# Cross attention: value products by head pairs, with high and low V columns in one stationary, and half of the softmax sums on VectorE

## The chip, the cores and the metric

One core of one Trainium2 chip runs the whole problem in one launch. The metric is device time in microseconds (us); lower is better.

## The reference

For each of 32 batches there are 512 queries of width 640 and 77 context rows of width 1024. Queries, keys and values are projected, 20 heads of 32 columns attend to the 77 context rows (all 77 are text rows, so the other branches of the original layer are empty), and the result is projected, with bias and residual added.

```python
q = heads(x @ to_q_w)                                   # (32, 20, 512, 32)
k, v = heads(ctx @ to_k_w), heads(ctx @ to_v_w)         # (32, 20, 77, 32)
s = einsum('bhqd,bhkd->bhqk', q, k) / sqrt(32)
p = softmax(s, axis=-1)
h = merge(einsum('bhqk,bhkd->bhqd', p, v))              # (32, 512, 640)
out = h @ to_out_w + to_out_b + x
```

## The kernel before

**Numbers.** All operands are fp32. TensorE multiplies fp32r values, so each operand is split into a high part (a cast to fp32r) and a low part (the rest), and a product is the sum of three: high by high, high by low, low by high. `PAIRS` lists them.

**Context stage.** The 2464 context rows are taken in five groups of 512 (the last has 416). For each group, keys and values of the five column chunks (128 columns, four heads each) are made with eight accumulation steps per chunk. `split_values` transposes a chunk of V in 32 by 32 blocks on VectorE (`vt`), splits it into high and low in the tile `vs` (two buffers: ScalarE casts, VectorE subtracts), and issues four DMAs to `v_dram` on SyncE's queue (L235). The order on ScalarE is that of the program: in groups 1 to 4, the casts of the next group's context (`ct`) of steps 1 and up stand behind the `vs` cast of chunk 3.

**Main stage.** A slot `n` handles one chunk `j` of one batch `b` (160 slots). The order of all engines is written out by hand in `slot`; every engine takes its instructions in that order. In a slot,
- TensorE makes four score tiles (`scores`, three matmuls each, t = 0 to 3, three PSUM buffers), the queries of the next slot (`queries`, 6 + 9 matmuls of 512 columns), the value product of slot n - 3 (`values`), and two pieces of output projection of the batch before (`piece`, 12 matmuls of 320 columns each).
- VectorE takes the negated row maxima of each score tile (`nm`, L482); ScalarE makes 16 exponentials of 128x77 with them (`exps`, L492), each of which also gives its row sum in `sm` by `accum_out`; VectorE inverts the sums of slot n - 1 (`rs`, L502); GpSimd multiplies (`pn`, L507); VectorE transposes (`z`, L514); SyncE stores `z` to `pd` (L521) and loads it back two slots later with keys on partitions (`raw`).
- ScalarE casts the probabilities of slot n - 3 (`pp`, L538 and L544), VectorE makes the low parts of their first 256 rows (L545), and GpSimd those of the last 64 rows (L552), which lie with their high parts in `pp[:, 4]`.
- `values` (L566) contracts over 320 rows: four heads of 80 padded keys. Its stationary `vb` is block diagonal: 128 rows by the 32 columns of each of four heads. It takes eight passes of 512 columns: three for rows 0 to 127, three for rows 128 to 255, and two for rows 256 to 319, where high and low probabilities share one operand, `pp[:, 4]`.
- `split_a` splits the product into `at` (ScalarE L104, VectorE L105), which the projection (`project`, L596) takes a batch later. VectorE adds the residual and bias, which GpSimd has added up in `xr` (L589), to a closed output bank (`finish`, L624).
- `transpose_x` (VectorE L257) and `split_x` (ScalarE L264, GpSimd L265) prepare the next batch's `x` in some of the slots: transposes after t = 1 in j = 1 and 2, transposes between the last score tile and `split_a` in j = 0 and 1, casts in j = 2 and 3.

The order at the end of a slot is this:

```python
        if taken is not None:
            values(taken)
        ...
            s = scores(n, 3)
        finish()
        for i in turns[1]:
            transpose_x(b + 1, i)
        if taken is not None:
            split_a(taken)
        for c in xsplits[1]:
            split_x(b + 1, c)
        exps(n, 3, *s)
```

The next slot begins with `cast_p` on ScalarE.

Of the kernel before, what the change touches and what calls it, by code (L numbers as in the profile page):

```python
# [23 lines left out]
P = 128  # L24
# [11 lines left out]
SEGMENTS = []  # L36
for _t in range(3):
    for _i in range(HPC):
        _lo = max(_t * P, _i * KPAD)
        _hi = min((_t + 1) * P, (_i + 1) * KPAD)  # L40
        if _lo < _hi:
            SEGMENTS.append((_t, _lo - _t * P, _i, _lo - _i * KPAD, _hi - _lo))
            if _t == 2:
                SEGMENTS.append((_t, _lo - _t * P + 64, _i, _lo - _i * KPAD, _hi - _lo))

# [5 lines left out]
def kernel(  # L51
# [46 lines left out]
    v_dram = dram.tile([NT + KPAD - NKEY, HPC, NC_, HD, 2], FPR, name="v_dram")  # L98
# [124 lines left out]
    def split_values(g, j, between=None):  # L223
# [7 lines left out]
        vs = kvp.tile([P, G // Q, HD, 2], FPR, tag="vs", name="vs", bufs=2)  # L231
        split(vs[:, :na, :, 0], vs[:, :na, :, 1], vt[:, :gn].rearrange("p (a d) -> p a d", d=HD))
        dst = v_dram[g0 : g0 + gn, :, j].rearrange("(a t) i d c -> i t a (d c)", t=Q)
        for i in range(HPC):
            nc.sync.dma_start(  # L235
                dst[i].bitcast(F32),
                vs[i * Q : (i + 1) * Q, :na].rearrange("p a d c -> p a (d c)").bitcast(F32),
            )
# [31 lines left out]

    zero = kvt.tile([P, 2, G], FPR, name="zero", tag="ks")[:, 0]
# [45 lines left out]
    def split_wo():  # L317
# [8 lines left out]
        v_dram[NT:].rearrange("n i j d a -> (n i j d a)").rearrange("(p u) -> p u", u=P).bitcast(F32),  # L326
        zero[: (KPAD - NKEY) * HEADS * HD * 2 // P, :P].bitcast(F32),
# [62 lines left out]
    raws, pps, ats, pds, sms, pqs, pas, xrs, pos = ({} for _ in range(9))  # L390
# [14 lines left out]
    for g, (j0, nj) in enumerate(GROUPS):  # L405
        vb = main.tile([P, nj, 3, HPC * HD, 2], FPR, name=f"vb{g}")
        nc.gpsimd.memset(vb.bitcast(F32), 0.0)
        vbs.append(vb)
# [12 lines left out]
    def load_values(b, g, segments=SEGMENTS):  # L421
        j0, nj = GROUPS[g]
        v = v_dram.rearrange("n i j d a -> n j i (d a)")
        for t, r0, i, k0, kn in segments:
            k0 += b * NKEY
            nc.sync.dma_start(
                vbs[g][r0 : r0 + kn, :, t, i * HD : (i + 1) * HD, :]
                .rearrange("p j d a -> p j (d a)")
                .bitcast(F32),
# [57 lines left out]
    def exps(n, t, sc, nm):  # L487
        if t == 0:
            sms[n] = main.tile([P, NQ * HPC], F32, tag="sm", name="sm", bufs=2)
        for i in range(HPC):  # L490
# [6 lines left out]
                accum_out=sms[n][:, at : at + 1],  # L497
            )

# [11 lines left out]
    def transpose_p(n):  # L511
# [6 lines left out]
        pd = dram.tile([NBLK * Q, S], F32, tag="pd", name="pd", bufs=6)  # L518
        rows = pd.rearrange("(b i) q -> i b q", i=Q)
# [7 lines left out]
    def load_p(n):  # L527
        pd = pds.pop(n)
        raw = late[0].tile([P, 3, S], F32, tag="raw", name="raw", bufs=2)
        nc.sync.dma_start(raw[:, 0:2, :], pd[0 : 2 * P, :].rearrange("(k p) q -> p k q", p=P))  # L530
        nc.sync.dma_start(raw[:64, 2, :], pd[2 * P :, :])
# [26 lines left out]
    PASSES = [(t, a, t + c * 2) for t in range(2) for a, c in PAIRS] + [(2, 0, 4), (2, 1, 4)]  # L558

    def values(n):  # L560
# [3 lines left out]
        pas[n] = late[1].tile([P, S], F32, tag="pa", name="pa", bufs=1)  # L564
        for m, (t, a, c) in enumerate(PASSES):
            nc.tensor.matmul(  # L566
                pas[n],
                vb[:, t, :, a],
                pp[:, c, :],
                start=(m == 0),  # L570
                stop=(m == len(PASSES) - 1),
            )

    def split_a(n):
# [4 lines left out]
        split(at[:, 0, :], at[:, 1, :], pas.pop(n))  # L579
# [11 lines left out]
    def output_bank(b, t, h):  # L591
        pos[b, t, h] = late[1].tile([P, S], F32, tag="po", name="po", bufs=3)
# [14 lines left out]
    STEPS += [(t, h, j) for t in range(1, NQ) for h in range(2) for j in range(NC_)]  # L607
    closed = []

    def piece(b, i):  # L610
        for t, h, j in STEPS[4 * i : 4 * i + 4]:
# [36 lines left out]
    def take(m):  # L648
        values(m)
        split_a(m)  # L650
# [248 lines left out]
```

## Time and profile before

| what | value |
| --- | --- |
| time, median of 3 runs (lowest to highest) | 1958.72 us (1957.45 to 1960.53) |
| span of the profiled execution, first to last instruction | 1956.4 us |
| mean granted TensorE clock | 0.997 |
| TensorE busy | 1929.6 us (99%) |
| ScalarE busy | 1596.1 us (82%) |
| VectorE busy | 1363.1 us (70%) |
| GpSimd busy | 1024.9 us (52%) |
| share of the 16 DMA engines, hardware queue of SyncE | 83.4% |

The profiled execution has no time of its own in the runs; its span is 2.3 us below the median of the runs, and that difference is taken for what lies around the span. The stretches of the profile are the context stage (0 to 262 us), the first slots, in which nothing is projected yet (262 to 396 us), the main stage (396 to 1915 us) and the end (1915 to 1957 us). "Idle before" in a row is the time in which that engine waited just before the instruction, and the arrow names what ended it.

### The profile page before, as it was taken

Reading aid. Unit: us, or ns where it says so; the run is one execution under the profiler, and the core shown is the slowest. Engines: PE = TensorE matmul, PEld = TensorE weight load, DVE = VectorE, ACT = ScalarE, POOL = GpSimd, SP = SyncE. Lnnn points to the kernel's source line nnn. Section 1 sums busy time; section 2 is a strip of 40 time slices with the busy share of each in tenths; the row PEclk is TensorE's granted clock in tenths of the full one; section 3 lists DMA queues with packets and bytes.
Section 4 is the critical chain, followed back from the end, with each engine's and each line's share of the span. In section 5 each row is a group of like instructions: output and inputs, shape, how many; then the busy total and the mean of one; then the engine's idle time right before and its main releaser. Section 6 shows DMA issues by size and latency. Waiting matters only on the chain.

```text
span 1956.4 us, 37549 instructions
## 1 busy us (share of the span) xinstructions
PE 1929.6 (99%) x10652; PEld 1727.8 (88%) x10652; DVE 1363.1 (70%) x2174; ACT 1596.1 (82%) x6370; POOL 1024.9 (52%) x688
## 2 busy tenths in 40 slices
PE   9999997999999999999999999999999999999999
PEld 7787895889989989999999999999999999998998
DVE  4444446677777777777777777777777777777774
ACT  3232248899999999999999999999999999999993
POOL 0211144566556555555555556655655565555555
PEclk9999999999999999999999999999999999999999
DMA  9877869988888889888988888888888888888876
GB/s 187 172 166 214 174 158 209 219 231 227 216 220 226 227 222 233 226 226 224 236 219 235 217 232 226 226 222 234 223 227 225 225 221 228 218 223 226 224 205 190
DMA packets 592537, 423.49 MB, mean 216 GB/s; under 512 B 219567, under 2 KB 501325, under 8 KB 592333
## 3 DMA queue, kind: packets, MB, share of 16 engines
q1 hardware_dynamic: 588461, 409.79, 83.4%
q0 software_dynamic: 3776, 11.15, 2.1%
q8 instruction: 88, 1.44, 0.3%
q14 instruction: 116, 0.95, 0.2%
q10 hardware_dynamic: 96, 0.16, 0.0%
HBM read 245.61 MB, written 175.32 MB: 215 GB/s over the span
## 4 chain that ended last, share of the span: by engine, by line
PE 86%; DMA 6%; SPq 2%; ACT 2%; DVE 2%; issue 2%; POOL 1%; ACTq 0%; DVEq 0%; POOLq 0%
PE po L596 27%; PE pq L439 26%; PE pa L566 14%; PE sc L474 10%; PE pk L192 5%; PE pv L192 4%; DMA raw<-pd 2%; DMA xs<-in_x_dram 1%; DMA pd<-z 1%; SPq L235 1%; DMA k_dram<-ks 1%; POOL pn L507 1%; ACT pp L538 0%; DMA v_dram<-vs 0%; ACT pn L492 0%
## 5 line engine op out<-in xcount | busy, mean ns | idle before, releaser
L492 ACT ACTIVATE pn<-sc,nm 128x77 f32<-128x77 f32 x2560 | 799.2, 329 | 45.2 <-DVE nm L482 32.4
L507 POOL TENSOR_TENSOR pn<-pn,rs 128x1232 f32<-128x1232 f32 x160 | 364.7, 2279 | 646.9 <-DVE rs L502 632.9
L596 PE MATMUL po<-wo_s,at 128*128 128x320 f32 x3840 | 625.9, 312 | 0.1
L439 PE MATMUL pq<-xt,wq_s 128*128 128x512 f32 x2400 | 619.3, 398 | 1.2 <-POOL xt L265 1.2
L596 PEld LDWEIGHTS po<-wo_s,at 128*128 128x128 f32 x3840 | 565.0, 188 | 0.7 <-DVE xr L624 0.3
L492 ACT ACTIVATION_READ_ACCUMULATOR pn<-sc,nm 128x1 f32 x2560 | 529.5, 207 | 0.0
L482 DVE TENSOR_REDUCE nm<-sc 128x4 f32<-128x308 f32 x640 | 294.2, 460 | 308.8 <-PE sc L474 303.9
L439 PEld LDWEIGHTS pq<-xt,wq_s 128*128 128x128 f32 x2400 | 428.4, 189 | 78.3 <-POOL xt L265 2.4
L566 PE MATMUL pa<-pp,vb 128*128 128x512 f32 x1280 | 329.3, 398 | 2.8 <-POOL pp L552 2.4
L566 PEld LDWEIGHTS pa<-pp,vb 128*128 128x128 f32 x1280 | 242.3, 196 | 43.0 <-POOL pp L552 5.3
L514 DVE STREAM_TRANSPOSE z<-pn 128x1280 f32<-128x1280 f32 x160 | 241.3, 1508 | 27.5 <-POOL pn L507 20.9
L545 DVE TENSOR_TENSOR pp<-raw,pp 128x1024 fp32r<-128x1024 f32 x160 | 196.1, 1226 | 71.3 <-ACT pp L538 63.9
L474 PEld LDWEIGHTS sc<-kc,qt 128*128 128x128 f32 x1280 | 211.6, 188 | 26.6 <-ACT qt L454 4.6
L552 POOL TENSOR_TENSOR pp<-raw,pp 64x512 fp32r<-64x512 f32 x160 | 210.5, 1316 | 42.5 <-ACT pp L544 30.6
L474 PE MATMUL sc<-kc,qt 128*128 128x154 f32 x1280 | 223.0, 255 | 4.1 <-DVE qt L456 2.1
L456 DVE TENSOR_TENSOR qt<-pq,qt 64x512 fp32r<-64x512 f32 x320 | 214.5, 670 | 11.7 <-ACT qt L450 7.3
L265 POOL TENSOR_TENSOR xt<-xs,xt 128x512 fp32r<-128x512 f32 x160 | 204.1, 1296 | 32.3 <-ACT xt L264 28.3
L589 POOL TENSOR_TENSOR xr<-xr,bias 128x640 f32<-128x640 f32 x128 | 201.2, 1573 | 9.7
L454 ACT CAST qt<-qt 64x512 fp32r<-64x512 f32 x320 | 198.1, 619 | 9.0
L474 PE MATMUL sc<-kb,qt 128*128 128x308 f32 x640 | 195.3, 305 | 7.4 <-ACT pn L492 6.2
L538 ACT CAST pp<-raw 128x1024 fp32r<-128x1024 f32 x160 | 170.2, 1064 | 17.3 <-DMA raw<-pd 17.1
L104 ACT CAST at<-pa 128x512 fp32r<-128x512 f32 x160 | 94.7, 592 | 75.8 <-PE pa L566 75.4
(44 smaller groups left out, 1542.5 us busy)
## 6 DMA issues: line engine op xcount, KB each, us to landing
pd<-z SPq DMA_DIRECT2D x640, 160.0 KB, 3.5
raw<-pd SPq DMA_DIRECT2D x160, 512.0 KB, 4.3
xs<-in_x_dram SPq DMA_DIRECT2D x128, 320.0 KB, 6.3
xr<-in_x_dram SPq DMA_DIRECT2D x128, 320.0 KB, 3.8
out_dram<-xr SPq DMA_DIRECT2D x127, 320.0 KB, 3.1
raw<-pd SPq DMA_DIRECT2D x160, 128.0 KB, 4.4
v_dram<-vs SPq DMA_DIRECT2D x80, 128.0 KB, 3.0
kc<-k_dram SPq DMA_DIRECT2D x128, 57.8 KB, 4.2
```

The source lines that it names most:

```text
L265: low.tensor_tensor(parts[1], src, parts[0].bitcast(F32), ALU.subtract)
L439: nc.tensor.matmul(pqs[n], wq_s[:, k, a, j * P : (j + 1) * P], xts[b, k][:, c, :], start=(k == 0 and m == 0), stop=(k == NC_ - 1 and m == 2),)
L456: nc.vector.tensor_tensor(qt[r, 1 + w, :], pq[r], qt[r, 0, :].bitcast(F32), ALU.subtract)
L474: nc.tensor.matmul(sc[:, cols], qt[:, m, t * P : (t + 1) * P], keys_, start=(m == 0), stop=(m == 2),)
L482: nc.vector.tensor_reduce(nm, sc[:, :KCOLS].rearrange("p (h k) -> p h k", k=NKEY), AX.X, ALU.max, negate=True)
L492: nc.scalar.activation(pnb[n % 2][:, at, :NKEY], sc[:, i * NKEY : (i + 1) * NKEY], AF.Exp, bias=nm[:, i : i + 1], accum_out=sms[n][:, at : ...
L507: nc.gpsimd.tensor_tensor(pf, pf, rs.unsqueeze(2).to_broadcast([P, NQ * HPC, NKEY]), ALU.mult)
L514: nc.vector.transpose(z.rearrange("p b t j -> p t b j"), pn.rearrange("p (t h) k -> p t (h k)", t=NQ).rearrange("p t (b i) -> p t b i", i=Q),)
L552: nc.gpsimd.tensor_tensor(pp[64:, 4, :], raw[:64, 2, :], pp[:64, 4, :].bitcast(F32), ALU.subtract)
L566: nc.tensor.matmul(pas[n], vb[:, t, :, a], pp[:, c, :], start=(m == 0), stop=(m == len(PASSES) - 1),)
L589: nc.gpsimd.tensor_tensor(xrs[b, t], xrs[b, t], bias, ALU.add)
L596: nc.tensor.matmul(pos[b, t, h][:, :HALF], ats[b * NC_ + j][:, a, t * P : (t + 1) * P], wos[0][:, j, c, h * HALF : (h + 1) * HALF], start= ...
```

## The change

1. **V by head pairs.** The 320 rows are regrouped into three sets of 128, 128 and 64: one set for heads 0 and 1, one for heads 3 and 2, and a shared set with the rest of heads 1 and 2. `vb` holds for each pair p a stationary of 128 columns: 64 of high and 64 of low V columns of the two heads. `values` takes three passes for each pair (high probabilities, low probabilities, shared set), six in all, into two PSUM banks (`pa`, 128 x 2 x 512); low by low is now part of the product. The third pass of the first pair reads `pp[:, 4]`.
2. **Adding the parts.** `sum_a`, new, copies the 64 low rows of `pa` (64 x 1024) to SBUF on ScalarE, and VectorE adds them to the high rows, two adds of 64x512. `split_a` casts from SBUF on ScalarE, and its subtraction goes from VectorE to GpSimd. It stands behind `exps(n, 3)`.
3. **Sums.** The exponentials of t = 0 and 1 no longer give sums; VectorE sums their 8 x 77 columns (`reduce_sums`, one reduction a slot, behind `sum_a`).
4. **Around it.** `vs` is one tile for the whole kernel in place of two buffers, with a zero column block between high and low, so `v_dram` rows are 96 numbers in place of 64. The output banks are two in place of three; the pieces of the projection are cut at other steps (`CUTS`), and in slots with j = 3 `finish` comes ahead of the last score tile too. `pd` has a gap of 64 rows so that `raw` lands in the new grouping.

```diff
-        vs = kvp.tile([P, G // Q, HD, 2], FPR, tag="vs", name="vs", bufs=2)
-        split(vs[:, :na, :, 0], vs[:, :na, :, 1], vt[:, :gn].rearrange("p (a d) -> p a d", d=HD))
+        split(vs[:, :na, 0], vs[:, :na, 2], vt[:, :gn].rearrange("p (a d) -> p a d", d=HD))
...
+    vs = kvp.tile([P, G // Q, 3, HD], FPR, name="vs")
+    nc.gpsimd.memset(vs.bitcast(F32), 0.0)
...
-        vb = main.tile([P, nj, 3, HPC * HD, 2], FPR, name=f"vb{g}")
+        vb = main.tile([P, nj, 2, 2, P], FPR, name=f"vb{g}")
...
                 bias=nm[:, i : i + 1],
-                accum_out=sms[n][:, at : at + 1],
-            )
+                **({} if t in REDUCED else dict(accum_out=sms[n][:, at : at + 1])),
+            )
+
+    REDUCED = (0, 1)
+
+    def reduce_sums(n):
+        k = len(REDUCED) * HPC
+        nc.vector.tensor_reduce(sms[n][:, :k], pnb[n % 2][:, :k, :NKEY], AX.X, ALU.add)
...
-    PASSES = [(t, a, t + c * 2) for t in range(2) for a, c in PAIRS] + [(2, 0, 4), (2, 1, 4)]
+    PASSES = [(p, t, c) for p in range(2) for t, c in ((0, p), (0, 2 + p), (1, 4))]
...
-        pas[n] = late[1].tile([P, S], F32, tag="pa", name="pa", bufs=1)
-        for m, (t, a, c) in enumerate(PASSES):
+        pas[n] = late[1].tile([P, 2, S], F32, tag="pa", name="pa", bufs=1)
+        for m, (p, t, c) in enumerate(PASSES):
             nc.tensor.matmul(
-                pas[n],
-                vb[:, t, :, a],
+                pas[n][:, p, :],
+                vb[:, p, t, :],
                 pp[:, c, :],
-                start=(m == 0),
-                stop=(m == len(PASSES) - 1),
+                start=(m % 3 == 0),
+                stop=(m % 3 == 2),
             )
+
+    def sum_a(n):
+        pa = pas.pop(n)
+        aw = late[0].tile([P, 2, S], F32, tag="aw", name="aw", bufs=1)
+        nc.scalar.copy(aw[:64], pa[64:])
+        for p in range(2):
+            nc.vector.tensor_tensor(aw[64 * p : 64 * p + 64, 0], pa[:64, p], aw[:64, p], ALU.add)
+        aws[n] = aw
...
-        split(at[:, 0, :], at[:, 1, :], pas.pop(n))
+        aw = aws.pop(n)
+        nc.scalar.copy(at[:, 0, :], aw[:, 0])
+        nc.gpsimd.tensor_tensor(at[:, 1, :], aw[:, 0], at[:, 0, :].bitcast(F32), ALU.subtract)
...
-        pos[b, t, h] = late[1].tile([P, S], F32, tag="po", name="po", bufs=3)
+        pos[b, t, h] = late[1].tile([P, S], F32, tag="po", name="po", bufs=2)
...
+    CUTS = (0, 4, 8, 10, 16, 20, 24, 28, 32, 36, 40)
...
             values(taken)
         ...
+        if j == 3:
+            finish()
         if has_out:
             s = scores(n, 3)
         finish()
         for i in turns[1]:
             transpose_x(b + 1, i)
         if taken is not None:
-            split_a(taken)
+            sum_a(taken)
+        reduce_sums(n)
         for c in xsplits[1]:
             split_x(b + 1, c)
         exps(n, 3, *s)
+        if taken is not None:
+            split_a(taken)
```

## The prediction

> **What bounds the kernel now.** I read the page first: busy times and the shares of the chain that ended last.
>
> ```profile
> PE 1929.6 (99%) x10652; PEld 1727.8 (88%) x10652; DVE 1363.1 (70%) x2174; ACT 1596.1 (82%) x6370; POOL 1024.9 (52%) x688
> ...
> PE 86%; DMA 6%; SPq 2%; ACT 2%; DVE 2%; issue 2%; POOL 1%; ACTq 0%; DVEq 0%; POOLq 0%
> ```
>
> TensorE is the bound, and by the stretches it is so in the main stage almost without a gap: 1518.14 us busy of the 1519 from 396 to 1915. The chain in order of time gives its price list:
>
> ```profile
> 1011.79 0.33 PE sc L474 x3
> 1012.11 1.80 PE po L596 x12
> 1013.91 1.87 PE pa L566 x8
> ```
>
> A value pass is 1.87 / 8 = 0.235 us, and a slot is 10.3 us (51.5 a batch). A shorter TensorE helps only if the other engines can follow, so I next read the timeline of one slot (j = 1), for the ring of waits that runs from one `pp` cast (L538) to the next.
>
> ```profile
> 1007.82 1.05 ACT L538 CAST pp<-raw 128x1024 fp32r<-128x1024 f32 x1
> ...
> 1008.90 1.23 DVE L545 TENSOR_TENSOR pp<-raw,pp 128x1024 fp32r<-128x1024 f32 x1 [0.35 <-ACT pp L538]
> ...
> 1010.04 0.25 DVE L502 RECIPROCAL rs<-sm 128x16 f32<-128x16 f32 x1
> ...
> 1010.43 2.28 POOL L507 TENSOR_TENSOR pn<-pn,rs 128x1232 f32<-128x1232 f32 x1 [5.22 <-DVE rs L502]
> ...
> 1012.74 1.51 DVE L514 STREAM_TRANSPOSE z<-pn 128x1280 f32<-128x1280 f32 x1
> 1012.79 1.29 POOL L552 TENSOR_TENSOR pp<-raw,pp 64x512 fp32r<-64x512 f32 x1
> 1013.75 2.04 PE L566 MATMUL pa<-pp,vb 128*128 128x512 f32 x8
> ...
> 1014.18 1.37 DVE L456 TENSOR_TENSOR qt<-pq,qt 64x512 fp32r<-64x512 f32 x2
> ...
> 1015.82 0.59 ACT L104 CAST at<-pa 128x512 fp32r<-128x512 f32 x1 [0.69 <-PE pa L566]
> ...
> 1016.15 0.48 DVE L482 TENSOR_REDUCE nm<-sc 128x4 f32<-128x308 f32 x1 [0.60 <-PE sc L474]
> 1016.66 0.49 DVE L624 TENSOR_TENSOR xr<-po,xr 128x320 f32<-128x320 f32 x1
> 1017.07 0.83 DVE L257 STREAM_TRANSPOSE xs<-xs 128x640 f32<-128x640 f32 x1
> ```
>
> In the middle of the list: the low part L552 is done at 1014.08, 0.3 us into the value passes, and only the last two of eight read it. The first `pp` cast to the end of that row takes 6.26 us, each step released by the one before. After it nothing in the ring is long today: `at` cast, exponentials of t = 3 (1.2 us, four at 0.30), next cast at 1017.88. TensorE has room over it because VectorE's part of `at` (L105) is not in the ring.
>
> **The change, part by part.** Its own time: span 1956.4, 2.3 us outside, median 1958.7. All differences are put on the median. I take start-to-start distances where steps follow each other.
>
> *Two passes fewer.* 2 x 0.235 = 0.47 us a slot of TensorE, 10.31 to 9.84, if TensorE stays the bound. The stage holds 1519 / 51.5 = 29.5 batches: -2.35 x 29.5 = -69 us.
>
> *The ring with the parts added.* Time 0 is the start of L538. From the rows above: L545 at 1.08, `rs` at 2.22, `pn` at 2.61, `z` at 4.92, L552 from 4.97 to 6.26. Now the third pass of six reads `pp[:, 4]`, so four passes, not two, stand behind L552: first pass to `at` cast was 2.07 us for eight, less 4 x 0.235 = 1.13, so `pa` is complete at 6.28 + 1.13 = 7.41. The 64x1024 PSUM copy is not in the trace. Between its neighbours, the 128x1024 cast from SBUF (1.06) and 0.59 for 512 PSUM columns, both ends are 0.98 to 1.1; I take 1.03, from the row of equal length. The two adds have the shape of the `qt` rows (64x512, one PSUM operand): 1.37. Then the `at` cast, and 0.53 later (L544 to its successor is 0.52) the next L538. The new waits stand in queues: ScalarE's copy waits for `pa` as its cast did, with t = 3 behind it; the `at` cast now waits for VectorE, with L538 and so the whole next turn behind it; the third value pass waits for GpSimd, with the last scores and the projection behind it.
> - Through `pa` alone: 7.41 + 1.03 + 0.03 + 1.37 + 0.03 + 0.53 = 10.40 us.
> - Through VectorE, which has `z` and `qt` first: `z` 4.92, `qt` 6.36 to 7.73, `nm` of t = 3 at 7.74 (its scores follow `values` on TensorE), 0.45 to `xr`, 0.40 to the adds at 8.59, L538 at 8.59 + 1.37 + 0.03 + 0.53 = 10.52. That is j = 4.
> - j = 0 and 1 have a transpose (0.76) ahead of the adds: 11.28.
> - j = 2 has an `xt` cast (0.52) behind the copy, so ScalarE decides: 7.41 + 0.93 + 0.52 + 1.21 (t = 3) + 0.53 = 10.60.
> - j = 3: ScalarE has three `xt` casts: t = 1 waits for `rs` and `nm` to 2.83, 0.87 for it, `qt` casts 1.91, t = 2 1.21, two casts 1.04, copy at about 7.9, then 0.93 + 0.52 + 1.21 + 0.53: 11.08. The `xr` rows moved ahead of `nm` there end before it.
>
> A batch is 10.52 + 2 x 11.28 + 10.60 + 11.08 = 54.8 us against 51.5; 29.5 x 3.3 = **+97 us**. The ring passes through every slot, so the gain on TensorE becomes waiting for L552, 0.5 to 1.4 us a slot. If the VectorE rows of j = 0 and 1 should fit ahead of the copy's end after all, a batch is 3 x 10.40 + 10.60 + 10.6 to 11.08, 52.4 to 52.9: +27 to +41.
>
> *Sums on VectorE.* The sum row starts 0.215 us into an exponential and the next exponential 0.30 after it: eight save 0.7 us of ScalarE a slot, which the copy takes back. Only one group of four lies in a ring (j = 3). The reduction (616 SBUF columns; the 308-column `nm` takes 0.46, so 0.5 to 0.9) lies between the adds and the next L545, where 1.6 us are free: nothing. It delays `nm` of t = 0 to about the end of L544; cover gone, it would cost up to 0.3 a slot. [...]
>
> *Subtraction on GpSimd.* 160 more of 1.30 us. GpSimd waits 5.2 us in this slot for `rs`. In j = 3 its list is fullest: `pn` 2.36, L552 1.37, `xr` 1.56, three `xt` and the new one at 1.30 each, 10.5 of a slot of 11.08. Nothing; if the cover of 0.6 us were gone, the next `pn` and with it the ring would move one for one.
>
> *Two output banks.* One slot in five (j = 3) may wait 0.5 us for `xr` rows on TensorE: hidden in the ring's slack.
>
> *One `vs` buffer.* The context stage has no slack: TensorE is busy 254.6 of 262 us, and a next group's `ct` casts stand behind the `vs` cast of chunk 3.
>
> ```profile
> 111.87 0.67 ACT L104 CAST vs<-vt 128x512 fp32r<-128x512 f32 x1
> ...
> 118.92 0.65 ACT L104 CAST vs<-vt 128x512 fp32r<-128x512 f32 x1 [0.85 <-DMA v_dram<-vs]
> ...
> 122.21 0.65 ACT L104 CAST vs<-vt 128x512 fp32r<-128x512 f32 x1 [1.26 <-DMA v_dram<-vs]
> ```
>
> A buffer comes back at the earliest after cast 0.65, subtraction 0.7, four issues of 0.5 and 2.8 to land: 6.2 us; the rows show 6.2 to 8.3 (with 256 KB in flight; 192 KB now). I take 6.5. Three turns after the first cast, chunk 3 is cast at 75 instead of 68.3; at 131 instead of 122.2 (0.7 us of it free, as TensorE needs the next `ct` at 126.3, then done by 125.6); at 185 instead of 179.4; at 238 instead of 229.4 (3.4 free): 6.5 + 8.5 + 5.5 + 5 = **+26 us**, with 22 to 47 for turns of 6.2 to 8.3. No gain is possible here: a buffer is removed and bytes are added.
>
> *Rest.* First slots, paced by ScalarE (`pp` casts 9.5 to 12.4 apart): the longer ring, +4 (0 to 8). End: cast and subtraction 1.3 us behind the last `pa` become 1.03 + 1.37 + 0.6 + 1.3 = 4.4, of which 12 matmuls (1.8) hide part, less 0.5: +3. Wider `v_dram` rows: 14 MB more of 423, same packets, in stretches where DMA is at 0.87: nothing by itself.
>
> Sum: 97 + 26 + 4 + 3 = +130, 1958.7 to **2088 us**.
>
> **Rivals.** *The ring gives way and TensorE stays the bound* (faster): -69 + 26 + 4 + 3 gives 1923. For it: 99% busy and six passes for eight. Against it: it needs 0.6 us less in every one of the measured steps' sums, even through `pa` alone (10.40 against 9.84). It decides when a ring falls below 9.84. *The weak ring* (slower): only the way through `pa` counts, 52.4 to 52.9 a batch, +34 + 26 + 7 gives 2025; it needs VectorE's rows from `z` to the adds to come out 0.1 us (j = 4) to 0.9 us (j = 0 and 1) shorter than the trace has them. *No change* needs gain and loss to meet: a ring of 10.1 us, between the two rivals, for which no row speaks.
>
> The gaps of TensorE raise one more danger. From 262 to 396 us it was busy 119.6 of 134 us, and the granted clock stayed 0.97. [...] By the row the stage keeps its clock, with gaps of 0.5 to 1.4 us, and nothing is added for it.
>
> **How the numbers follow.** Forecast 0.70, its own range 2050 to 2130; weak ring 0.20, 2000 to 2050; TensorE-bound 0.08; no change 0.02. The range of 8 in 10 is 2010 to 2130. A measurement can tell 0.2% (4 us): faster 0.08, same 0.02, slower 0.90.
>
> **What would show it.** Right: `pa` waits on GpSimd `pp` in most slots, TensorE near 90% busy, batches of 54 to 55 us, `at` cast waiting for VectorE, and `vs` casts waiting for DMA in all groups. Wrong: TensorE at 99% again, or 49.2 us a batch.

## The result and the profile after

The changed kernel takes 2231.98 us (median of four runs, 2228.06 to 2233.01) against 1959.62 (four runs, 1957.45 to 1962.01): a ratio of 1.1387, interval 1.1369 to 1.1405. It is slower by 272 us; the forecast was +130, and the time lies above its range. This is the first row of the page after, to set beside the same row of before. TensorE has the same work less two passes a slot, and yet it is busy for 28 us more (1929.6 before), in a span 12% of which it has nothing to do.

```profile
PE 1957.6 (88%) x10332; PEld 1701.7 (76%) x10332; DVE 1623.6 (73%) x2494; ACT 1646.0 (74%) x5250; POOL 1223.5 (55%) x849
```

Where the 274.8 us between the two spans (1956.4 and 2231.2) lie is read from the `pp` casts on ScalarE (L538 before, L545 after), one a slot:

| stretch | before | after | difference | predicted |
| --- | --- | --- | --- | --- |
| start to the first `pp` cast | 303.7 | 369.9 | +66.2 | +26 |
| first three batches of casts | 157.2 | 172.1 | +14.8 | |
| next 27 batches | 1392.1 | 1566.9 | +174.9 | +89 (3.3 each) |
| the rest to the last instruction | 103.4 | 122.3 | +18.9 | |

A batch in the middle takes 58.03 us instead of 51.56, +6.5 where +3.3 was predicted. By slots, j = 3, 4, 0, 1, 2: 11.53, 12.08, 11.66, 11.67, 11.10 us, against a forecast of 11.08, 10.52, 11.28, 11.28, 10.60. The windows of the trace by stage give the same picture. The columns are the stretch, its length, the busy time of PE, PEld, DVE, ACT and POOL, the granted clock, the DMA share and GB/s:

```profile
0.00:262.00 262.00, 216.35 (x901) 175.25 (x902) 95.80 (x149) 62.78 (x107) 36.48 (x70) 0.92 0.76 169
425.38:2108.86 1683.48, 1508.49 (x8269) 1323.59 (x8268) 1361.96 (x2090) 1423.59 (x4641) 1063.67 (x696) 0.97 0.84 205
```

In the first 262 us TensorE is busy for 216.35 us, where it was 254.60 at a clock of 0.99. In the main stage no engine is busy all the time: TensorE 90%, ScalarE 85%, VectorE 81%. That is a ring of waits, not a bound by work. TensorE's busy time there is 52.0 us a batch, where two passes a slot less should have left 49.2. Part of it is the clock: its mean of 0.97 is full clock but for one stretch of 3.41 us at half clock in each of the 27 batches, at the end of the slot j = 3. Two of these stretches, with the time between them, in the same columns (the third number from the end is the granted clock):

```profile
550.00:553.41 3.41, 3.00 (x11) 3.01 (x12) 3.29 (x6) 3.36 (x12) 3.41 (x4) 0.50 0.97 217
553.42:608.02 54.60, 49.00 (x276) 42.68 (x274) 43.55 (x67) 45.60 (x150) 33.17 (x22) 1.00 0.83 204
608.03:611.43 3.40, 2.93 (x12) 2.90 (x12) 3.28 (x6) 3.35 (x12) 3.40 (x4) 0.50 0.97 206
```

In the kernel before there is none in these 27 batches. The table of waits (engine, line, releaser; total us, times, longest) names its links:

```profile
PEld pa L573 <- POOL pp L559: 223.3, 128, 3.1
PE pa L573 <- POOL pp L559: 159.0, 122, 2.6
ACT vs L105 <- DMA v_dram<-vs: 92.0, 14, 9.4
ACT at L595 <- DVE aw L586: 73.9, 95, 1.5
```

The first two are the third value pass waiting for the low part on GpSimd, the fourth is the `at` cast waiting for the adds: both were forecast. The third is the single `vs` buffer. The timeline of one slot (j = 0) shows the ring that the prediction built from the trace of before, now as it ran:

```profile
1320.11 1.05 ACT L545 CAST pp<-raw 128x1024 fp32r<-128x1024 f32 x1
...
1320.29 1.29 POOL L596 TENSOR_TENSOR at<-aw,at 128x512 fp32r<-128x512 f32 x1 [3.65 <-ACT at L595]
...
1321.19 1.47 DVE L552 TENSOR_TENSOR pp<-raw,pp 128x1024 fp32r<-128x1024 f32 x1 [0.48 <-ACT pp L545]
...
1321.58 0.95 ACT L493 ACTIVATE pn<-sc,nm 128x77 f32<-128x77 f32 x4
...
1322.58 0.24 DVE L509 RECIPROCAL rs<-sm 128x16 f32<-128x16 f32 x1
...
1322.90 2.27 POOL L514 TENSOR_TENSOR pn<-pn,rs 128x1232 f32<-128x1232 f32 x1 [1.32 <-DVE rs L509]
...
1325.25 1.27 POOL L559 TENSOR_TENSOR pp<-raw,pp 64x512 fp32r<-64x512 f32 x1
...
1326.58 1.20 PE L573 MATMUL pa<-pp,vb 128*128 128x512 f32 x4 [0.84 <-POOL pp L559]
...
1326.64 1.35 DVE L457 TENSOR_TENSOR qt<-pq,qt 64x512 fp32r<-64x512 f32 x2
...
1327.87 1.01 ACT L584 COPY aw<-pa 64x1024 f32<-64x1024 f32 x1 [0.58 <-PE pa L573]
...
1328.14 0.48 DVE L483 TENSOR_REDUCE nm<-sc 128x4 f32<-128x308 f32 x1
1328.65 0.49 DVE L642 TENSOR_TENSOR xr<-po,xr 128x320 f32<-128x320 f32 x1
...
1329.06 0.83 DVE L257 STREAM_TRANSPOSE xs<-xs 128x640 f32<-128x640 f32 x1
...
1329.81 1.34 DVE L586 TENSOR_TENSOR aw<-pa,aw 64x512 f32<-64x512 f32 x2
...
1331.24 0.62 ACT L595 CAST at<-aw 128x512 fp32r<-128x512 f32 x1 [1.01 <-DVE aw L586]
...
1331.77 1.04 ACT L545 CAST pp<-raw 128x1024 fp32r<-128x1024 f32 x1
```

Every step is there in the order forecast, and the slot ends as the sum had it: adds, `at` cast, 0.53 us, next cast. But it is 0.38 us late, and about half of that arises at the third line. L552 takes 1.47 us where it took 1.23: the new subtraction on GpSimd (second line) has just been released by the `at` cast and runs until 1321.58. What stands behind L552 moves with it: `rs` at 2.47 instead of 2.22, the low part at 5.14 instead of 4.97. The other half arises behind the low part, in the four value passes that wait for it: the copy comes at 7.76 instead of 7.41. In j = 4 the ring looks different: L552 starts 1.86 us after its cast, when the subtraction on GpSimd is over, and takes 1.22 us.

### The profile page after: what moved, and what is told of

The parts are those of the page before. It is cut to its first block, busy times and chain, and to the rows that moved or that the text cites. A ratio compares the mean times of both kernels' runs of the same rounds, so it can differ in the third digit from the quotient of the medians.

```text
span 2231.2 us, 36333 instructions
## 1 busy us (share of the span) xinstructions
PE 1957.6 (88%) x10332; PEld 1701.7 (76%) x10332; DVE 1623.6 (73%) x2494; ACT 1646.0 (74%) x5250; POOL 1223.5 (55%) x849
## 5 line engine op out<-in xcount | busy, mean ns | idle before, releaser
L493 ACT ACTIVATE pn<-sc,nm 128x77 f32<-128x77 f32 x2560 | 706.7, 324 | 134.7 <-DVE nm L483 126.8
L613 PE MATMUL po<-wo_s,at 128*128 128x320 f32 x3840 | 677.5, 328 | 26.0 <-DVE xr L642 22.2
L613 PEld LDWEIGHTS po<-wo_s,at 128*128 128x128 f32 x3840 | 606.3, 201 | 41.3 <-DVE xr L642 36.2
L596 POOL TENSOR_TENSOR at<-aw,at 128x512 fp32r<-128x512 f32 x160 | 206.9, 1293 | 439.1 <-ACT at L595 279.9
L573 PE MATMUL pa<-pp,vb 128*128 128x512 f32 x960 | 286.2, 412 | 169.0 <-POOL pp L559 159.0
L573 PEld LDWEIGHTS pa<-pp,vb 128*128 128x128 f32 x960 | 164.1, 188 | 243.2 <-POOL pp L559 223.3
L521 DVE STREAM_TRANSPOSE z<-pn 128x1280 f32<-128x1280 f32 x160 | 241.5, 1509 | 118.8 <-POOL pn L514 66.2
L552 DVE TENSOR_TENSOR pp<-raw,pp 128x1024 fp32r<-128x1024 f32 x160 | 229.1, 1432 | 75.5 <-ACT pp L545 75.5
L493 ACT ACTIVATION_READ_ACCUMULATOR pn<-sc,nm 128x1 f32 x1280 | 259.9, 203 | 0.0
L586 DVE TENSOR_TENSOR aw<-pa,aw 64x512 f32<-64x512 f32 x320 | 216.1, 675 | 28.0 <-ACT aw L584 23.4
L584 ACT COPY aw<-pa 64x1024 f32<-64x1024 f32 x160 | 161.8, 1011 | 69.5 <-PE pa L573 66.5
```

The source lines that it names most:

```text
L493: nc.scalar.activation(pnb[n % 2][:, at, :NKEY], sc[:, i * NKEY : (i + 1) * NKEY], AF.Exp, bias=nm[:, i : i + 1], **({} if t in REDUCED el ...
L521: nc.vector.transpose(z.rearrange("p b t j -> p t b j"), pn.rearrange("p (t h) k -> p t (h k)", t=NQ).rearrange("p t (b i) -> p t b i", i=Q),)
L552: nc.vector.tensor_tensor(pp[:, 2:4, :], raw[:, 0:2, :], pp[:, 0:2, :].bitcast(F32), ALU.subtract)
L573: nc.tensor.matmul(pas[n][:, p, :], vb[:, p, t, :], pp[:, c, :], start=(m % 3 == 0), stop=(m % 3 == 2),)
L586: nc.vector.tensor_tensor(aw[64 * p : 64 * p + 64, 0], pa[:64, p], aw[:64, p], ALU.add)
L613: nc.tensor.matmul(pos[b, t, h][:, :HALF], ats[b * NC_ + j][:, a, t * P : (t + 1) * P], wos[0][:, j, c, h * HALF : (h + 1) * HALF], start= ...
```

## The experiments

All but the last are single runs, each beside the kernel before (1957.6 to 1962.7 us there). They are read by their `pp` casts as above. "Batch" is the mean of the same 27 batches. Context stages of equal code put the first cast anywhere from 323.2 to 331.8 us (six kernels with two `vs` buffers), so differences of less than 10 us in all are not read.

**Two `vs` buffers in the changed kernel.** Two weight buffers in place of three make room for it.

```diff
-    vs = kvp.tile([P, G // Q, 3, HD], FPR, name="vs")
+    vss = [kvp.tile([P, G // Q, 3, HD], FPR, name=f"vs{i}") for i in range(2)]
```

> The changed kernel with two vs buffers (both with the zero block), and two instead of three wraw buffers to make room. Theory (one buffer makes ScalarE wait for the stores of the V chunk before, with the next context casts behind it): chunk 3 of each group is cast 10 to 20 us earlier again, the first pp cast comes at 305 to 320 us instead of 370, and the time falls by 50 to 65 us, to 2167 to 2182; the main stage stays at 58.0 us a batch. Rival (the wider v_dram rows, 192 KB a chunk, are slow by themselves): the turn stays at 7 us or more and less than 20 us come back.

2185.86 us: 46 less. The first cast comes at 323.9 instead of 369.9, the batch stays at 58.02.

**One `vs` buffer in the kernel before.**

```diff
-        vs = kvp.tile([P, G // Q, HD, 2], FPR, tag="vs", name="vs", bufs=2)
+        vs = kvp.tile([P, G // Q, HD, 2], FPR, tag="vs", name="vs", bufs=1)
```

> The kernel before, with one vs buffer in place of two and nothing else. Theory (the buffer alone makes ScalarE wait): chunk 3 of each group is cast later, the first pp cast moves from 304 to 335 to 350 us, the main stage stays at 51.5 us a batch, and the time is 1990 to 2010. Rival (it needs the 96-number rows as well): less than 15 us more.

1999.58 us: 42 more; the first cast comes at 347.6 instead of 303.7, the batch is 51.50. One buffer costs 42 to 46 us in either kernel. The first cast at 323.9 with two buffers is still 20 us later than before. It is not the two weight buffers: with one `vs` buffer and three weight buffers in both kernels the difference is 22 us (369.9 against 347.6). That leaves the wider rows of `v_dram`, whose stores (L235 before) take 3.9 us to land in place of 3.0, but no run has these alone. The timeline of ScalarE in the second group of the changed kernel shows the turn of the buffer, and TensorE's shows what it does to the next group:

```profile
128.00 0.62 ACT L105 CAST vs<-vt 128x512 fp32r<-128x512 f32 x1
...
137.06 0.62 ACT L105 CAST vs<-vt 128x512 fp32r<-128x512 f32 x1 [4.91 <-DMA v_dram<-vs]
144.21 0.62 ACT L105 CAST vs<-vt 128x512 fp32r<-128x512 f32 x1 [5.12 <-DMA v_dram<-vs]
151.32 0.62 ACT L105 CAST vs<-vt 128x512 fp32r<-128x512 f32 x1 [5.10 <-DMA v_dram<-vs]
```

```profile
154.04 11.13 PE L193 MATMUL pk<-ct,wk_s 128*128 128x512 f32 x40 [11.66 <-ACT ct L105]
```

A turn is 7.1 to 9.1 us here and up to 10.6 in the other groups; TensorE then waits 11.66 us for the `ct` casts that stand behind the fourth `vs` cast. The granted clock is half from 147.2 to 157.5 us, and the 40 matmuls take 11.13 us, where 40 of them take 9.23 at full clock.

**Shared passes last.**

```diff
-    PASSES = [(p, t, c) for p in range(2) for t, c in ((0, p), (0, 2 + p), (1, 4))]
+    PASSES = [(0, 0, 0), (1, 0, 1), (0, 0, 2), (1, 0, 3), (0, 1, 4), (1, 1, 4)]
```

> The changed kernel with the two passes over the shared set (pp[:, 4]) moved behind the other four, so that two passes instead of four stand behind the GpSimd subtraction. Ring theory: 0.47 us less in the slots in which TensorE waits for that subtraction (four of five), less where it does not, so 1.9 to 2.4 us a batch of 58.0, 55 to 70 us in all, to 2162 to 2177. Rival (the added work of VectorE, ScalarE and GpSimd sets the pace, not the order): no change, 2225 to 2235.

2230.58 us, batch 57.96: nothing in the time. The copy did start 0.45 us earlier (7.30), but the adds only 0.1 earlier. In j = 0 and 1 VectorE reaches them no sooner, with `z`, `qt`, `nm`, `xr` and a transpose ahead of them; in j = 2 ScalarE's own row is full. The way through `pa` alone does not set the slot, which is against the weak ring among the rivals. The equal batch is no evidence for that, the slots are: 26 of the 27 batches of this run have the half clock, 58.03 us apart, and the one without it takes 56.63. In the changed kernel too it comes every 58.03 us, which is 17 stretches of 3.41 us, and the batches of several kernels of different order stay at that length.

**No reduction on VectorE**: all exponentials give their sums again.

```diff
-    REDUCED = (0, 1)
+    REDUCED = ()
```

> The changed kernel with all exponentials giving their sums and no reduction on VectorE. Theory (the reduction lies in VectorE's free time behind the adds and costs nothing; the sums cost ScalarE 0.35 us more for each of the tiles t = 0 and 1, of which only t = 1 lies in the way of the copy): 0 to 2 us more a batch, 2230 to 2290. Rival (VectorE is too full, and the reduction's 0.8 us a slot is what stretched the ring): 40 to 120 us less.

2234.11 us, batch 58.03: nothing on balance. By slots, j = 0 and 1 do not change (11.66, 11.67), so the reduction costs nothing there; j = 3 and 2 are longer by 0.37 and 0.32, so the sums saved on ScalarE do gain there; and j = 4, behind the half clock, is shorter by 0.70, which keeps the batch at 58.03.

**The low part of `at` on VectorE again**, in its place behind the cast.

```diff
-        nc.gpsimd.tensor_tensor(at[:, 1, :], aw[:, 0], at[:, 0, :].bitcast(F32), ALU.subtract)
+        nc.vector.tensor_tensor(at[:, 1, :], aw[:, 0], at[:, 0, :].bitcast(F32), ALU.subtract)
```

> The changed kernel with the at subtraction back on VectorE. Theory that GpSimd's subtraction, which runs beside VectorE's pp low part, slows it from 1.23 to 1.47 us inside the ring: the mean falls back from 1.43 to 1.23 us, about 0.1 to 0.2 us a slot come back after what the subtraction itself now takes on VectorE ahead of it: 2200 to 2225. Rival (the longer row has another cause, such as the operands): it stays at 1.43, and the time rises to 2235 to 2300 since VectorE has 0.65 us more in its ring.

2191.53 us: 40 less, batch 56.66. The group of L552 has 1432 ns as its mean in the changed kernel, and here (busy us, mean ns; then idle before):

```profile
L552 DVE TENSOR_TENSOR pp<-raw,pp 128x1024 fp32r<-128x1024 f32 x160 | 194.3, 1215 | 2.9 <-ACT pp L545 2.9
```

That is more than was expected, and only half of it is L552. In j = 3, 0, 1 and 2 the slots are 0.13 to 0.23 us shorter, 0.69 a batch together: VectorE has 0.7 us more work a slot, but no longer runs L552 beside the same subtraction on GpSimd. The other 0.69 is in j = 4, and it is TensorE's clock: the half clock comes in only nine of the 27 batches. Two batches of this run, first the clock as above, then the 18 projection matmuls at the end of j = 3:

```profile
549.62:553.01 3.39, 3.25 (x12) 3.26 (x13) 3.15 (x7) 3.37 (x12) 3.39 (x3) 0.50 0.94 234
665.00:945.00 280.00, 253.03 (x1423) 221.08 (x1424) 242.80 (x385) 244.47 (x800) 150.82 (x95) 1.00 0.86 212
```

```profile
549.76 4.37 PE L613 MATMUL po<-wo_s,at 128*128 128x320 f32 x18 [0.48 <-DVE xr L642]
...
665.09 2.91 PE L613 MATMUL po<-wo_s,at 128*128 128x320 f32 x18 [0.47 <-DVE xr L642]
```

The slot j = 4 behind them takes 12.37 us in the nine batches with half clock and 10.90 in the 18 without; the other slots agree within 0.03 us.

**The projection cut evenly.**

```diff
-    CUTS = (0, 4, 8, 10, 16, 20, 24, 28, 32, 36, 40)
+    CUTS = (0, 4, 8, 10, 14, 18, 22, 27, 31, 36, 40)
```

> The changed kernel with CUTS = (0, 4, 8, 10, 14, 18, 22, 27, 31, 36, 40): the second projection piece of a slot with j = 3 has 12 matmuls in place of 18. Theory (the long piece and the wait for an output bank ahead of it make the scores of j = 4 late, and VectorE's pp low part stands behind their maxima): the slot of j = 4 falls from 12.1 to 11.2 to 11.5 us, 18 to 27 us in all, 2205 to 2214. Rival (j = 4 is long for another reason): no change.

2211.16 us: 21 less, batch 57.17; the slot j = 4 falls from 12.08 to 11.10, the others stay. In the changed kernel j = 4 begins with its t = 0 scores late: the piece in j = 3 has 18 matmuls, waits 0.43 us for one of the two output banks and takes 4.14 us at half clock; VectorE's `nm` of t = 0 waits for those scores, and L552, behind `nm`, starts 1.86 us after its cast instead of 1.08. With 12 matmuls in the piece the half clock (in 20 of the 27 batches here) costs little: j = 4 is 11.13 with it and 11.01 without. At full clock the long piece and its wait cost j = 4 nothing that can be read: 10.90 us with 18 matmuls in the run before this one, 10.88 with 12 in the next.

**The three undone together**: two `vs` buffers, the low part on VectorE, even cuts.

```diff
+    vss = [kvp.tile([P, G // Q, 3, HD], FPR, name=f"vs{i}") for i in range(2)]
...
+        nc.vector.tensor_tensor(at[:, 1, :], aw[:, 0], at[:, 0, :].bitcast(F32), ALU.subtract)
...
+    CUTS = (0, 4, 8, 10, 14, 18, 22, 27, 31, 36, 40)
```

> The changed kernel with three of its side edits undone together: two vs buffers, the low part of `at` on VectorE, the projection cut evenly. Single effects were -46, -40 and -21 us. Theory: they sit in different places (context stage; L552 beside GpSimd; the late scores of j = 4) and add up: 2125 us (2115 to 2135), batches of 55 us, and what is left above the kernel before is the copy and the adds in the ring. Rival: the last two shorten the same wait, and only one of them counts: 2145 us or more, batches of 56 us or more.

2151.44 us, batch 56.31: the rival's case in time and batch. The `vs` buffers add up with the rest, but the subtraction (-1.4 a batch) and the cuts (-0.9) give -1.7 together, not -2.3: both take what the half clock costs out of j = 4. The 19 batches at full clock take 56.15 us here, and the 18 with only the low part moved took 56.16. What is left, 56.31 against 51.56, is the adding with its order, the six passes and the reduction.

**`at` one slot later**: the cast behind the next slot's `pp` casts and the subtraction behind GpSimd's `pp` row, except in j = 2.

```diff
+        back_ = held.pop() if held else None
+        if back_ is not None:
+            high_a(back_)
...
+            if j == 2 or n + 2 >= N:
+                split_a(taken)
+            else:
+                held.append(taken)
```

> The changed kernel with the at cast moved from the end of a slot behind the pp casts of the next slot, and its GpSimd subtraction behind that slot's pp subtraction (not in slots with j = 2 and at the end, which stay as they are). Ring theory: the pp cast no longer waits for the two adds; what remains is VectorE's own ring (pp low part, sums, z, qt, maxima, xr, adds, reduction), 11.2 us in j = 0 and 1 and 10.4 to 10.8 else, so 2 to 3 us less a batch, 60 to 90 us in all, to 2142 to 2172; the pp low part falls back to 1.23 us where the GpSimd subtraction no longer runs beside it. Rival (work, not order): no change.

2231.2 us, batch 57.99: nothing on balance, but not for lack of an effect. Four slots are shorter (11.26, 10.85, 10.26, 10.92), and j = 2 takes 14.69, since the projection there already needs the `at` that now comes later (TensorE waits for it 32 times, 2.8 us on the mean), and in 17 of the 27 batches the half clock falls there (15.19 with it, 13.85 without).

**All reordered, low part on VectorE**: two `vs` buffers, shared passes last, even cuts, the `at` cast a slot later with VectorE's subtraction behind `nm` of t = 1, the reduction ahead of `z`, transposes of `x` earlier.

```diff
+    def low_a(n):
+        aw, at = aws.pop(n), ats[n]
+        nc.vector.tensor_tensor(at[:, 1, :], aw[:, 0], at[:, 0, :].bitcast(F32), ALU.subtract)
...
+    TRANSPOSE_X = {0: ((0,), (), ()), 1: ((1,), (), ()), 2: ((2, 3), (), ())}
...
         s = scores(n, 1)
+        if back_ is not None:
+            low_a(back_)
...
-            split_a(taken)
+            held.append(taken)
```

> The changed kernel with its order repaired: two vs buffers (two wraw), shared passes last, the even cuts, at cast behind the next slot's pp casts with its subtraction on VectorE behind the maxima of t = 1, the reduction ahead of z, where VectorE waits for GpSimd, and the transposes of x there too. All arithmetic stays as in the changed kernel. Ring theory: no ring is above 10 us any more, a batch takes 49.5 to 51.5 us, the first pp cast comes at about 324, and the time is 1925 to 1985. Rival (the engines' added work sets the pace whatever the order): a batch stays above 54 us, over 2050.

2281.47 us, batch 60.80: far from the theory, and slower even than the changed kernel. The time is in the rival's range. The timelines of GpSimd and of VectorE show one cause:

```profile
1020.34 2.28 POOL L517 TENSOR_TENSOR pn<-pn,rs 128x1232 f32<-128x1232 f32 x1 [5.84 <-DVE rs L512]
```

```profile
1020.58 2.59 DVE L609 TENSOR_TENSOR at<-aw,at 128x512 fp32r<-128x512 f32 x1
```

The subtraction took 0.69 us at its old place (1096.95 in the kernel with three edits undone), and takes 2.59 beside `pn` here, and 2.58 on the mean of all slots.

**The same with the low part on GpSimd**, behind its `pp` row, and the projection's steps and cuts arranged for the later `at`.

```diff
+    STEPS = [(0, h, j) for h in range(2) for j in range(3)]
+    STEPS += [(0, h, j) for j in (3, 4) for h in range(2)]
...
+    CUTS = (0, 4, 8, 8, 10, 15, 20, 25, 30, 35, 40)
```

> As the run with everything reordered, but the at subtraction stays on GpSimd, behind that slot's pp subtraction, so that no VectorE instruction with two SBUF operands runs beside pn; and the projection's steps are taken in another order (chunks 0 to 2 first, then 3, then 4, pieces of 4, 4, 0, 2, 5, 5, 5, 5, 5 and 5 steps), so that the later at is not waited for. [...] Rival (the added work sets the pace whatever the order): a batch stays above 54 us, over 2050.

2088.61 us, batch 54.59. That is in the rival's range and far above the 1925 to 1985 us that the ring theory gave for the run before, yet 143 us below the changed kernel, all of it by order and one buffer, so the work alone does not hold the changed kernel at 58 us. How much of the step from 60.80 is the subtraction and how much the projection's new order was not parted. In j = 0 (12.64 us) VectorE stands 2.74 us at a transpose of `x`. The row names no releaser, but 8 of the 30 such waits are put down to the load of `x`: the transposes had been put too early.

**The transposes of `x` back at their places.**

```diff
-    TRANSPOSE_X = {0: ((0,), (), ()), 1: ((1,), (), ()), 2: ((2, 3), (), ())}
+    TRANSPOSE_X = {0: ((), (0,), ()), 1: ((1,), (2,), ()), 2: ((3,), (), ())}
```

> The reordered kernel with GpSimd's low part, but with the transposes of x at their old places. In the reordered kernel (54.4 us a batch) the slot j = 0 took 12.5 us, since its transpose of x stood 2.7 us for its load. Theory: only that slot changes, to about 10.8: batches of 52.9 us, 2035 to 2060 us in all. Rival: the two output banks hold TensorE up in that slot, not the load: 54 us a batch or more, 2075 us or more.

2062.02 us, batch 53.51, j = 0 at 10.29: that fits the load, though j = 1 and 2 take back 1.3 of the 2.4 us gained, and the time is just above the range. This is the best version with six passes and the whole output, still 102 us above the kernel before: 27 until the first cast, 53 in the 27 batches, the rest at the two ends. The sequence of j = 4 there is worth a look, GpSimd's row first, then VectorE's:

```profile
1035.89 2.54 POOL L267 TENSOR_TENSOR xt<-xs,xt 128x512 fp32r<-128x512 f32 x2
```

```profile
1037.41 2.10 DVE L555 TENSOR_TENSOR pp<-raw,pp 128x1024 fp32r<-128x1024 f32 x1 [0.93 <-ACT pp L548]
```

**Scores of t = 3 ahead of the value passes**, and their exponentials ahead of the copy.

```diff
+        if has_out:
+            s = scores(n, 3)
         if taken is not None:
             values(taken)
...
+        exps(n, 3, *s)
         if taken is not None:
             sum_a(taken)
-        exps(n, 3, *s)
```

> As the kernel with the transposes back, but the scores of t = 3 stand ahead of the value passes on TensorE, and their exponentials ahead of the copy of `pa` on ScalarE. Theory: the ring is closed by the t = 3 scores that stand behind the value passes; with them ahead only the buffer of `pp` closes it (value passes end 7.9 us after the cast, then copy 1.0), and TensorE's six passes set the slot, 10.0 to 10.3 us: batches of 50.3 to 51.5 us, 1965 to 2000 us in all. Rival: the orders of VectorE and ScalarE are the limit: batches of 52.5 us or more, 2035 us or more.

2178.95 us, batch 57.21: longer by 3.7, so the rival holds and this theory falls. `nm` of t = 3 does not come earlier (8.60 us after the cast, right behind `qt`, which stands behind `z` and `pn`); and the adds now fall after the next cast, ahead of L555, which starts at 1.94 us.

**No adding.** The copy and the adds are left out and `at` is split from the first bank of `pa`.

```diff
-        aw = aws.pop(n)
-        nc.scalar.copy(at[:, 0, :], aw[:, 0])
-        nc.gpsimd.tensor_tensor(at[:, 1, :], aw[:, 0], at[:, 0, :].bitcast(F32), ALU.subtract)
+        split(at[:, 0, :], at[:, 1, :], pas.pop(n)[:, 0, :])
```

> The changed kernel without the adding of the parts: the copy and the two adds are left out, at is split straight from the first PSUM bank (ScalarE and VectorE, in the place it had in the kernel before), so the output lacks the second pair and the low V parts. Six passes, the reduction, the cuts and the single vs buffer stay. Theory (the adding and what waits for it is what stretched the ring; six passes by themselves are a gain): a batch takes 49.2 to 50.5 us, first pp cast at 370, 1958 + 62 - (30 to 65) = 1950 to 1995. Rival (the pass order or the reduction stretch it): above 53 us a batch, over 2070.

2027.24 us, batch 51.50, neither case. Nearly all that is above the kernel before is the context stage, with its first cast at 370.7 (67 later). The batch is that of eight passes, 51.56. In the windows, the same 27 batches of both kernels, this one first:

```profile
529.13:1919.63 1390.50, 1355.91 (x7698) 1201.49 (x7697) 1132.86 (x1810) 1197.15 (x4187) 820.97 (x514) 1.00 0.90 231
```

```profile
460.90:1852.97 1392.07, 1391.33 (x7968) 1261.42 (x7967) 1047.91 (x1674) 1282.69 (x5267) 823.99 (x514) 1.00 0.88 226
```

TensorE is busy for 35 us less, 1.3 a batch, and has turned all of it into waiting. Six passes gain nothing here even where adding costs nothing. The run keeps the reduction, the two banks and the 18-matmul piece, though, and that piece still holds j = 4 up at full clock: `nm` of t = 0 waits 1.24 us for its scores, L552 starts 1.52 us after its cast instead of 1.12, and the slot takes 10.58 us where it took 9.99 before. No run has six passes without adding and with even cuts.

**No adding, t = 3 early**: scores of t = 3 right behind those of t = 2, exponentials too.

```diff
         s = scores(n, 2)
+        early = ahead and has_out
+        s3 = scores(n, 3) if early else None
...
+        if early:
+            exps(n, 3, *s3)
```

> The kernel without the adding (as before it, it leaves out the copy and the adds, so the second head pair and the low V columns are missing from the output), with the scores of t = 3 right behind those of t = 2 on TensorE and VectorE, and their exponentials right behind those of t = 2. Without this move its batch was 51.43 us, as with eight passes, with TensorE busy 97.5%. Theory: the t = 3 scores, which stand behind the value passes, close the ring and hide the gain of two passes; moved ahead, a batch is what TensorE's work takes, 50.1 to 50.5 us, 1985 to 2000 us in all. Rival: another order (L545's wait for its cast, `pn` and `z`) holds it: 51.2 us or more, 2020 us or more.

2029.01 us, batch 51.62, TensorE busy 1348.2 of 1393.7 us: the rival again. It is not the t = 3 scores alone that hold six passes at 51.5.

**The kernel before, with the same move**, timed in three rounds.

```diff
         s = scores(n, 2)
+        early = ahead and has_out
+        s3 = scores(n, 3) if early else None
```

> The kernel before with the same move of the t = 3 scores and exponentials. Theory: TensorE is busy for the whole of its 51.45 us a batch with eight passes, so opening the ring brings nothing: 1955 to 1961 us. Rival: TensorE's busy time holds hidden waiting in the ring: 49.5 to 50.5 us a batch, 1900 to 1930 us.

1975.74 us against 1962.33, ratio 1.0083 (1.0055 to 1.0112), batch 52.01: neither theory's number, a loss of 0.8%. TensorE stays busy (1397.3 of 1404.2 us). The order of the kernel before is the better one with eight passes.

## Why the prediction was right and wrong

**Right:** that TensorE stops being the bound and the ring with copy and adds sets the slot; its links, in order, with the waits forecast (`pa` for GpSimd, `at` cast for VectorE, `vs` casts for DMA); and that VectorE's rows ahead of the adds count (the shared passes put last changed nothing). The copy was taken at 1.03 us and took 1.01; the two adds at 1.37 and took 1.34 to 1.38. The reduction was put at nothing, and costs nothing in j = 0 and 1, where VectorE's rows set the slot. Four exponentials without sums take 0.95 us, of which one is 0.33, so they follow each other every 0.21 us, close to the 0.215 that the prediction read from the row. TensorE at 90% is right by luck: 49.2 busy of 54.8 us were forecast, and it is 52.0 of 58.0.

**Wrong:** the size, +272 for +130. In the main stage a batch of 58.03 in place of 54.8 is, read from the runs with the low part on VectorE, 1.35 in the ring itself, 0.69 by the subtraction on GpSimd and 1.2 by the clock; the changed kernel itself has no batch at full clock. The steps that failed:

- *"By the row the stage keeps its clock ... nothing is added for it."* It does not keep it: half clock for 3.41 us in every batch, and j = 4 behind it was put at 10.52 us and took 12.08. At full clock j = 4 takes 10.90 (the 18 batches with the low part on VectorE), so this term, put at nothing, is worth 1.2 us a batch, some 35 us in all. The row was misread: its 0.97 was already two such stretches (329.3 to 332.7 and 343.0 to 346.4 us of the kernel before) and not a clock that stays. And the waits were put at 0.5 to 1.4 us, where that of j = 3 is 1.85.
- *"Subtraction on GpSimd. ... Nothing."* I looked only for room in GpSimd's list. The instruction runs beside L552 and makes it 1.47 us instead of 1.23 in four slots of five, and L552 is in their ring: 0.69 us a batch, 20 us in all. Undone alone it gives 40 us, since the half clock then goes from 18 of the 27 batches (the wait of the value passes in j = 3 falls from 1.85 to 1.66 us).
- *"Two output banks ... hidden in the ring's slack."* The wait was put at 0.5 us and is 0.43, and at full clock it is hidden, as forecast. But the cuts that came with the two banks put 18 matmuls into one piece, just where the half clock falls: 4.14 us instead of 2.91. I priced the wait on TensorE and did not follow who waits behind the piece (`nm` of t = 0, and L552 behind it). Even cuts alone give 21 us.
- *The ring with the parts added, +97.* With both undone the batch is 56.3, and 56.15 at full clock, not 54.8. From the end of GpSimd's low part to the copy, four restarted passes, it is 1.28 us in j = 1 there and was put at 1.15, so the copy comes at 7.55 to 7.59 and not at 7.41; `nm` of t = 3 follows the same passes, at 7.89 and not 7.74, and moves the adds. That is 0.25 us in four slots; j = 4 is 0.5 longer, and 0.36 at full clock. An error of 0.1 to 0.2 in one link counts 150 times.
- *"One `vs` buffer ... +26."* Measured 42 to 46. The turn was put at 6.5 us; it is 7 to 10.6. I had given the range (22 to 47) and took its low end for fewer bytes in flight, which was an estimate and is not borne out (the page has four stores of 192 KB a turn here, and of 128 KB before). At the waits for `ct` the clock was also half, 47.8 us in all against 13.7 with two buffers, for which the sum had nothing.
- *"Wider `v_dram` rows ... nothing by itself."* The first cast is 20 us later with two buffers too. That the rows alone do it was not tried; stores that take 3.9 us in place of 3.0 fit it, as a turn with two buffers still waits up to 6.7 us.
- *First slots +4, end +3.* The first three batches lost 14.8 us. From the last `pp` cast to the end it is 25.2 us and was 17.5: +8.
- *The rival "TensorE-bound", 1923, and the -69 us for two passes.* Had the adding been free, there would still have been no gain: 51.50 us a batch. So in this kernel, with its cuts, its reduction and four passes behind the low part instead of two, the other chains through the slot are as long as TensorE's work was with eight. The prediction's case for no gain was the longer ring with the adding; the ring without it is enough.

**Open:** what holds six passes at 51.5 us. It is neither the adds nor the t = 3 scores alone. In j = 4 the 18-matmul piece has a part in it, up to 0.6 us a batch; that beside it several orders of nearly one length meet (`nm` of t = 0 ahead of L552, `pn` ahead of `z`, `z` ahead of `qt`) is argued from the timelines and not shown. Also open is what makes the first `pp` cast 20 us late with two `vs` buffers.

## What to carry to other kernels

An engine at 99% does not tell that other chains are shorter: here TensorE's work fell by 1.3 us a batch without the adding, and the batch stayed at 51.50 us (51.56 before). Work taken from an engine is worth something only if every chain through the slot gets shorter by as much, and leaving out the new work (here the adding) showed that in one run. Moving an instruction to an engine with time to spare was not free here: beside GpSimd's subtraction, VectorE's L552 took 1.47 us instead of 1.22. So look at what runs at that moment, not at the engine's sum. Follow a wait one step further than the engine that waits: a long piece on TensorE was paid by VectorE, in the next slot (j = 4 took 12.08 us, and 11.10 with even cuts). And look at the clock by stretches and not by its mean: 0.97 was full clock with one half-clock stretch a batch, at the place where it cost most.

## What the hardware showed that was not expected

**Three VectorE instructions with both operands in SBUF took longer beside GpSimd's.** From the lines above: L552 ends 1.08 us after GpSimd's subtraction (1321.58 to 1322.66) and takes 1.22 us alone; L555 ends 1.08 us after GpSimd's `xt` rows (1038.43 to 1039.51) and took 1.21 alone in the run with all reordered; the subtraction of `at` ends 0.55 us after `pn` (1022.62 to 1023.17) and took 0.69 at its old place. In each of the three it is as if the instruction had begun when GpSimd's ended, less 0.13 to 0.14 us. In the changed kernel all 129 L552 that run beside the subtraction take 1.44 to 1.81 us and end 1.08 us after it; the 30 with nothing of GpSimd beside them take 1.21 to 1.22. The adds of `sum_a`, with one operand in PSUM, did not get longer: 122 of them run beside GpSimd's `xt` rows and take 0.68 us each, the other 198 take 0.64 to 0.69. What makes the difference was not shown.

**TensorE's clock was half behind stretches in which it stood still for about half of the time or more.** In the traces of the kernels before and after the granted clock is 1.00 or 0.50, and changes only at the ends of stretches of 3.41 us that follow each other through the whole run. In the changed kernel, from the first `pp` cast to the 156th, there are 494 such stretches at full clock. Behind 32 of them the clock is half, and in these TensorE was idle for 52% of the time or more; behind the other 462 it stays full, and in these TensorE was idle for 45% at most. In the kernel before, between the same casts, it is half behind two of 467 stretches (54% and 61% idle) and full behind the rest (46% at most). At the two ends of the changed kernel the cases overlap: half clock follows stretches with 47% and 50%, full clock two with 51% and 53%. All 32 stretches at half clock are followed by full clock; in them TensorE was idle for 14% at most. In each of the 27 batches the wait of j = 3, 1.85 us, falls into one stretch, and half clock follows; the longest wait, 1.92 us, begins 0.4 us ahead of the end of a stretch, and full clock follows. Batches of one run that differ (12.37 and 10.90 us in j = 4, with the low part on VectorE) fit this, as their 56.16 us is no whole number of stretches.

The same holds for the start of the main stage. Behind a wait of 4.15 us, the six query matmuls that take 1.59 us elsewhere took 2.85, with the clock at half from 324.7 to 331.5 us:

```profile
326.78 0.60 PE L475 MATMUL sc<-kb,qt 128*128 128x308 f32 x1 [4.15 <-ACT xt L264]
...
327.87 2.85 PE L440 MATMUL pq<-xt,wq_s 128*128 128x512 f32 x6
```

With waits of 7 to 15 us for `ct` in the context stage the mean clock is 0.92 instead of 0.99.
